# Attention and experts on one core: a large background piece between the two bursts of scores of a step

## The chip, the core and the metric

The kernel runs on one core of a Trainium2 chip. A core has five engines with a queue of instructions each: PE (TensorE, the matrix multiplier; its weight loads are shown apart as PEld), DVE (VectorE), ACT (ScalarE), POOL (GpSimd) and SP (SyncE, which here only issues DMAs). An engine works its queue in order and waits on semaphores for the others. Results of PE land in PSUM, from where DVE and ACT read them; a bank is here a tile of 128 partitions by 512 numbers of 32 bits, and the attention stage uses eight of them. The metric is the time of the kernel on the device in microseconds (us).

## The reference

One transformer layer in 32-bit floats on `x` of 8 batches x 1024 tokens x 256. First causal attention with 16 heads of 16 numbers, then a mixture of 8 experts of which each token uses two:

```python
x = x + layernorm(attention(layernorm(x), Wq, Wk, Wv, Wo))
x = x + layernorm(experts(layernorm(x), router, gate_up, down))

# attention, for each batch and head
score = q @ k.T / sqrt(16)              # 1024 x 1024
score = where(causal, score, -inf)
out = softmax(score) @ v
out = concat_of_heads(out) @ Wo.T

# experts
scores = softmax(flat @ router_weight.T + router_bias)
w, idx = top_k(scores, 2)
gate, up = split(flat @ gate_up[e] + bias[e])       # 512 each
act = (clip(up, -7, 7) + 1) * min(gate, 7) * sigmoid(1.702 * min(gate, 7))
out = sum over the two of w * (act @ down[e] + down_bias[e])
```

The change lies in the attention stage.

## The kernel before

The work of attention is cut into 32 units: 8 batches times 4 groups of 4 heads (`u` in the code, 0 to 31). Softmax needs the maximum of a row before its exponentials, so each unit is gone through twice. In the first pass (`maxima_tiles`, "first" in the loop) PE computes the scores with the queries on the partitions (`sa`, line 686), and DVE reduces them to row maxima (`mx`, lines 696, 702, 711, 717). The maxima are turned by PE (`nmps`, line 655), copied by ACT and put by four DMAs as one more row into the tile of queries (`qP`, line 659), so that the second pass subtracts them in the matrix product itself. In the second pass (`values_tiles`, "second") PE computes the scores again with the keys on the partitions (`sb`, line 781), ACT takes the exponentials (`pT`, line 789), POOL masks the diagonal blocks (line 798), and PE weights the values with them (`av`, line 818). The first pass of unit `u` runs together with the second pass of unit `u - 1`.

A unit has nine steps (`STEPS`, `k` from 0 to 8), which cover the lower triangle of 1024 x 1024 scores. Step kinds are EDGE (a tile with a diagonal block, two DVE reductions), TWO (two partial tiles, with copies by ACT and one more masked reduction) and WHOLE. Each step goes through two pairs of heads, so it has two half steps. A half step begins with a burst of scores: two heads of the first pass and two of the second, each on its own 32 of the 128 rows of PE, so that the four run side by side. Then come the exponentials and reductions of the burst, then half of a weighting: the columns 0 to 255 or 256 to 511 of the step that lies two steps back (`late`), four heads side by side in 32 columns of PE each. One call of `pump` ends the half step.

`pump` puts background work into the loop. This work is written as generators, jobs that yield a `piece` with the time that it is believed to cost PE, DVE, ACT and POOL, and the number of half steps until its input is believed to be ready (`after`). A piece is emitted when it is ready and no engine that it costs has a negative credit; each half step adds credit (0.68 us for PE, capped at 0.9). Three lists are searched in this order: `urgent` (`rows` with `nmps`, `masked_edges`, and `normalize` with `avt`, line 849), the first of `due` (layer norm and transposes of the next batch, its values `vps` in line 577, its projections `pjq` and `pjk` in line 591), then `back` (the output projection `yps` in line 877, the second layer norm, the routing and its scatters). Large pieces cost PE 1.75 us by the kernel's own figures: `vps`, `pjq`, `pjk` and `yps`. All other pieces that use PE are small, 0.6 us at most. Two deadlines, `finish_by`, emit what remains of a batch's values and projections.

The banks of PSUM set limits. `ps_a` has two buffers of two banks for `sa`; `ps_b` has three buffers of one bank, which `sb` (two in each half step), every large piece and every small piece of PE take in turn; `ps_v` has one for `av`. The order of PE, DVE, ACT and SP in the attention stage is the order in which the program emits, and POOL keeps it too (`in_order`).

The experts follow in 71 tiles of 256 tokens (`gu` line 1265, `dn` line 1296), with their own pumping of what is left of attention's last batch.

Of the kernel before, what the change touches and what calls it, by code (L numbers as in the profile page):

```python
# [58 lines left out]
def attn_moe_kernel(  # L59
# [345 lines left out]
    with ExitStack() as attn:  # L405
# [236 lines left out]
        def maxima_tiles(u):  # L642
# [82 lines left out]
            def counted_off(k):  # L725
                for c in {i // n for i, _, _ in STEPS[k][1]}:
                    left[c] -= 1
                    if not left[c]:
                        start(urgent, rows(c))

# [326 lines left out]

        urgent, due, back = [], [], []
        now = 0
        credit = [0.0] * 4  # L1060

        def start(kind, gen):
            job = Job(gen, now)
            kind.append(job)
            return job
# [11 lines left out]

        def pump(*us):

            nonlocal now  # L1080
            for i, more in enumerate(us):
                credit[i] = min(credit[i] + more, 1.3 if i == 3 else 0.9)
            found = True
            while found:
                found = False
                for kind, job in candidates():
                    if job.ready <= now and all(
                        not cost or has >= 0 for cost, has in zip(job.cost, credit)
                    ):
                        for i, cost in enumerate(job.cost):  # L1090
                            credit[i] -= cost
                        emit(kind, job)
                        found = True
                        break
            now += 1
# [22 lines left out]
        with tc.manual_schedule(  # L1118
# [10 lines left out]
            jobs["p1"] = start(due, project(0, 1))  # L1129
            second, late = None, deque()  # L1130
            for u in range(B * NG + 1):
                first = None
                if u < B * NG:
# [9 lines left out]
                    first = maxima_tiles(u)  # L1143
                for k in range(K):
                    if u == B * NG - 1 and not early and NT - LATE in known:
                        load_early()
                    if first and g == 0 and b + 1 < B and k == 5:
                        xs[b + 1] = load_x(b + 1)
                    if first and g == NG - 1 and b + 1 < B and k == K - 2:
                        finish_by(jobs["p0"])  # L1150
                        spread(u + 1)
                        jobs["v"] = start(due, values(b + 1))
                        jobs["p1"] = start(due, project(b + 1, 1))
                    for pair in range(2):
# [14 lines left out]
                        for _, use in reversed(heads):  # L1169
                            use()  # L1170
                        halves = (pair,) if first else (0, 1)
                        if len(late) > DELAY - 1 or (late and not second):
                            f, kk = late[0]
                            for half in halves:
                                f(kk, half)
                            if 1 in halves:
                                late.popleft()
                        if 1 in halves:
                            if first:
                                first[1](k)  # L1180
                            if second:
                                second[1](k)
                                late.append((second[2], k))
                        if first and second:

                            us = 1.64 + 0.62
                            of_dve = {WHOLE: 1.22, EDGE: 1.68, TWO: 0.72}[STEPS[k][0]]
                            of_act = 1.8 if STEPS[k][0] == TWO else 1.2
                            pump(0.68, us - of_dve, us - of_act, us - 0.35)
                        elif first:  # L1190
# [287 lines left out]
```

## Time and profile before

| | |
|---|---|
| Median of 3 runs | 2298.53 us (2292.19 to 2300.28) |
| The profiled execution's own time | 2275.28 us |
| Its span, from the first to the last instruction | 2273.4 us |
| Mean granted TensorE clock | 0.987 of full speed |
| PE busy | 2195.0 us, 97% |
| DVE, ACT, POOL busy | 72%, 48%, 47% |
| Large pieces `vps`, `yps` | 1.99 us each as drawn in the timeline |
| `sb` matmuls, line 781 | 720.0 us busy, 522 ns mean |
| `sa` matmuls, line 686 | 657.0 us busy, 526 ns mean |
| `av` matmuls, line 818 | 366.2 us busy, 368 ns mean |

The attention stage lies in the first 1435 us of the span, the experts in the rest. Each matmul of 32-bit numbers stands in the trace as two passes, so a count of 8 in a row of `av` is four heads. The matmuls of a burst run side by side, and the ends of matmuls are modelled, so the busy times above overlap; what the work takes on PE is read from the start of one group to the start of the next. A group of instructions in the page is given as line, engine, operation, output and input tiles, then busy time and mean duration, then the idle time of the engine before it and what ended that.

### The profile page before, as it was taken

The page shows a single profiled execution, that of the slowest core. Times are in us where ns is not written, and L with a number is a line of the kernel's source. Part 1 is how long each engine was busy: PE and PEld are TensorE (multiplying, and loading weights), DVE is VectorE, ACT ScalarE, POOL GpSimd, SP SyncE. Part 2 cuts the span into 40 slices and gives each one's busy share as a digit, 9 for nine tenths or more (in the row PEclk, how much of TensorE's full clock was granted, in tenths as well). Part 3 has the DMA queues.
Part 4 walks back from the last instruction along what each step waited for, and adds up shares of the span by engine and source line. Part 5 has one row for each costly group of instructions (what it writes and reads, how often), then busy time and mean ns, then how long its engine had stood idle before and what let it go on. Part 6 is the DMA issues. An engine that isn't in the chain of part 4 may idle for free.

```text
span 2273.4 us, 45180 instructions
## 1 busy us (share of the span) xinstructions
PE 2195.0 (97%) x16801; PEld 1363.7 (60%) x16801; DVE 1627.3 (72%) x3677; ACT 1091.8 (48%) x2181; POOL 1070.1 (47%) x1228
## 2 busy tenths in 40 slices
PE   7999999999999999999999999889999999999995
PEld 3444544444444444444445444677888888888884
DVE  4765777777777777777687686665557888887775
ACT  2565665665665666666656656431122323322222
POOL 3321463474364365365365354454444544554543
PEclk9999999999999999999999999999999999999998
DMA  3101102112012013012012010657667877878773
GB/s 81 39 2 39 21 21 58 28 32 58 12 39 48 21 30 86 12 33 55 21 29 58 21 39 30 230 179 221 202 216 256 281 256 268 269 248 279 244 249 110
DMA packets 149106, 251.05 MB, mean 110 GB/s; under 512 B 25920, under 2 KB 111832, under 8 KB 146840
## 3 DMA queue, kind: packets, MB, share of 16 engines
q1 hardware_dynamic: 134168, 210.86, 30.0%
q0 software_dynamic: 12960, 35.47, 4.3%
q8 instruction: 133, 2.18, 0.4%
q10 hardware_dynamic: 1760, 1.84, 0.3%
q14 instruction: 85, 0.70, 0.1%
HBM read 175.66 MB, written 55.68 MB: 102 GB/s over the span
## 4 chain that ended last, share of the span: by engine, by line
PE 83%; DVE 7%; POOL 4%; issue 3%; ACT 1%; DMA 1%; ACTq 0%; POOLq 0%; DVEq 0%; SPq 0%
PE sa L686 19%; PE gu L1265 18%; PE av L818 12%; PE dn L1296 10%; PE sb L781 8%; PE vps L577 3%; PE pjq L591 3%; PE pjk L591 3%; PE yps L877 3%; PE avt L849 1%; PE xtps L1249 1%; POOL pT L798 1%; DVE mx L702 1%; DVE mx L740 1%; DVE sa L696 1%
## 5 line engine op out<-in xcount | busy, mean ns | idle before, releaser
L789 ACT ACTIVATE pT<-sb 128x512 f32<-128x512 f32 x1152 | 625.1, 595 | 348.0 <-PE sb L781 316.8
L781 PE MATMUL sb<-qP,kP 32*128 32x512 f32 (+3 forms) x3072 | 720.0, 522 | 0.5 <-ACT pT L789 0.2
L686 PE MATMUL sa<-kP,qP 32*128 32x512 f32 (+3 forms) x3072 | 657.0, 526 | 6.2 <-DVE mx L702 3.0
L1265 PE MATMUL gu<-xsT,wg 128*128 128x256 f32 x2272 | 520.7, 382 | 2.5 <-ACT xsT L1251 2.5
L1265 PEld LDWEIGHTS gu<-xsT,wg 128*128 128x128 f32 x2272 | 433.9, 191 | 62.8 <-ACT xsT L1251 2.8
L798 POOL TENSOR_SCALAR_AFFINE_SELECT pT<-pT 128x512 f32<-128x512 f32 x256 | 160.3, 642 | 552.8 <-ACT pT L789 368.2
L702 DVE TENSOR_REDUCE mx<-sa 128x2 f32<-128x1024 f32 x256 | 311.5, 1219 | 140.9 <-PE sb L781 137.9
L1276 ACT ACTIVATE sig<-gate 128x256 f32<-128x256 f32 x284 | 118.3, 416 | 569.1 <-DVE gate L1274 540.2
L818 PE MATMUL av<-pT,vpad 128*32 128x256 f32 (+1 forms) x5120 | 366.2, 368 | 1.4 <-DVE avs L829 0.9
L686 PEld LDWEIGHTS sa<-kP,qP 32*128 32x128 f32 x3072 | 229.2, 184 | 207.8 <-issue 133.1
L1281 POOL TENSOR_TENSOR sig<-sig,gate 128x256 f32<-128x256 f32 x284 | 213.4, 753 | 279.8 <-ACT sig L1276 277.7
L781 PEld LDWEIGHTS sb<-qP,kP 32*128 32x128 f32 x3072 | 319.5, 184 | 30.0 <-ACT pT L789 4.6
L818 PEld LDWEIGHTS av<-pT,vpad 128*32 128x32 f32 x5120 | 106.1, 108 | 325.5 <-issue 277.1
L1296 PE MATMUL dn<-wd,act 128*128 128x256 f32 x1136 | 276.2, 384 | 14.1 <-DVE act L1286 14.1
L1274 DVE TENSOR_SCALAR gate<-gu,bs 128x256 f32<-128x256 f32 x284 | 136.0, 479 | 171.6 <-PE gu L1265 156.4
L1296 PEld LDWEIGHTS dn<-wd,act 128*128 128x128 f32 x1136 | 210.8, 192 | 46.5 <-DVE act L1286 21.0
L696 DVE CUSTOM_DVE_ANT_0 sa<-sa,cmask 128x512 f32<-128x512 f32 x256 | 178.3, 696 | 84.4 <-PE sb L781 62.3
L1306 POOL DMA_INDIRECT ytd<-ys,places x142 | 142.6, 1004 | 124.1 <-DVE ys L1302 96.5
L1044 POOL DMA_INDIRECT xsd<-xn,slots x128 | 128.2, 1002 | 107.2 <-DVE xn L1034 46.0
L711 DVE TENSOR_REDUCE mx<-sa 128x2 f32<-128x512 f32 x128 | 88.0, 687 | 88.4 <-PE sb L781 66.1
L1286 DVE SCALAR_TENSOR_TENSOR act<-up,sig 128x256 f32<-128x256 f32 x284 | 124.1, 437 | 21.4 <-POOL sig L1281 21.4
L1278 DVE TENSOR_SCALAR up<-gu,bs 128x256 f32<-128x256 f32 x284 | 134.6, 474 | 0.0
(198 smaller groups left out, 2390.3 us busy)
## 6 DMA issues: line engine op xcount, KB each, us to landing
wg<-_L_ffn_gate_up_proj_dram SPq DMA_DIRECT2D x71, 1024.0 KB
wd<-in_L_ffn_down_proj_dram SPq DMA_DIRECT2D x71, 512.0 KB
xs<-xsd SPq DMA_DIRECT2D x67, 257.0 KB
yy<-ytd SPq DMA_DIRECT2D x16, 1024.0 KB
bs<-biasd SPq DMA_DIRECT2D x71, 132.0 KB
x<-in_L_attn_x_dram SPq DMA_DIRECT2D x16, 512.0 KB
qP<-unq SPq DMA_DIRECT2D x128, 64.0 KB
x1d<-y SPq DMA_DIRECT2D x16, 512.0 KB
```

The source lines that it names most:

```text
L591: nc.tensor.matmul(ps, lhsT=wT[name][:, kt, ts(g2, P)], rhs=xnTs[b][:, kt, ts(c, QC)], start=(kt == 0), stop=(kt == KT - 1),)
L686: nc.tensor.matmul(ps[:, hh, ds(at, w)], lhsT=qP[r, ts(i, P)], rhs=kP[r, ds(c * QC, w)], start=True, stop=True,)
L696: nc.vector.tensor_tensor_reduce(out=ps[:, hh, :], in0=ps[:, hh, :], in1=cmask, scale=1.0, scalar=NEG, op0=ALU.add, op1=ALU.max, accum_out ...
L702: nc.vector.tensor_reduce(mx[:, heads, i, 2:3], ps, AX.X, ALU.max)
L781: nc.tensor.matmul(banks[hh][:, ds(at, QC - off)], lhsT=kP[r, ts(j, P)], rhs=qP[r, ds(c * QC + off, QC - off)], start=True, stop=True,)
L789: nc.scalar.activation(pT[:, 2 * pair + hh, :], banks[hh], AF.Exp)
L798: in_order(nc.gpsimd.affine_select(out=d, in_=d, compare_op=ALU.is_ge, fill=0.0, base=0, pattern=[[0, HG], [1, P]], channel_multiplier=-1,))
L818: nc.tensor.matmul(av[ds(hh * HS, HS), ds(off + a - at, z - a)], lhsT=vp[:, j, ds((g * HG + hh) * VS, HS)], rhs=pT[:, hh, a:z],  start=c n ...
L1265: nc.tensor.matmul(ps[:, half, :], lhsT=wg[:, kt, ds(half * FF + f * P, P)], rhs=xT[:, kt, :], start=(kt == 0), stop=(kt == KT - 1),)
L1281: in_order(nc.gpsimd.tensor_tensor(sg, sg, gt, ALU.mult))
L1296: nc.tensor.matmul(ps[:, n, :], lhsT=act[:, f, ts(n, P)], rhs=wd[:, f, :], start=(f == 0), stop=(f == FT - 1),)
L1306: put = nc.gpsimd.indirect_dma_start(out=yt_dram[:, :], out_offset=bass.IndirectOffsetOnAxis(ap=places[:, i, n : n + 1], axis=0), in_=y[:, ...
```

## The change

In a step with a large piece that can be afforded, the piece now stands between the step's two bursts of scores, where half a weighting stood, and the weighting that was due in the step stands whole behind the second burst. The weighting is kept in halves where it belongs to two chunks of queries (step 2 of a unit). Small pieces are emitted behind the weighting, as before, and large ones no longer are: while both passes run, `pump` takes pieces up to a PE cost of 1.0 only, and in a first half step whose weighting was put off it takes pieces without PE cost only. So there is at most one large piece in a step, always in its first half.

Three smaller edits come with it. Urgent pieces no longer need PE credit. Before each step of the second pass the row maxima that it needs are emitted if they were not yet (`rows_of`). The jobs that compute the next batch's values and its second projections are started at step 5 instead of step 7 of a batch's last unit.

```diff
-                        start(urgent, rows(c))
+                        rows_of[u, c] = start(urgent, rows(c))
...
+        rows_of = {}
...
-        def pump(*us):
-
-            nonlocal now
+        def earn(*us):
             for i, more in enumerate(us):
                 credit[i] = min(credit[i] + more, 1.3 if i == 3 else 0.9)
-            found = True
-            while found:
-                found = False
-                for kind, job in candidates():
-                    if job.ready <= now and all(
-                        not cost or has >= 0 for cost, has in zip(job.cost, credit)
-                    ):
-                        for i, cost in enumerate(job.cost):
-                            credit[i] -= cost
-                        emit(kind, job)
-                        found = True
-                        break
+
+        def affordable(least, most):
+            for kind, job in candidates():
+                if job.ready <= now and least <= job.cost[0] <= most and all(
+                    not cost or has >= 0 or (kind is urgent and not i)
+                    for i, (cost, has) in enumerate(zip(job.cost, credit))
+                ):
+                    return kind, job
+
+        def spend(least=0.0, most=9.0):
+
+
+            found = affordable(least, most)
+            if found:
+                kind, job = found
+                for i, cost in enumerate(job.cost):
+                    credit[i] -= cost
+                emit(kind, job)
+            return found is not None
+
+        def pump(*us, most=9.0):
+
+            nonlocal now
+            earn(*us)
+            while spend(most=most):
+                pass
             now += 1
...
                 for k in range(K):
+                    if second:
+
+                        for c in {t[0] for t in STEPS[k][2]}:
+                            while not rows_of[u - 1, c].done:
+                                emit(urgent, rows_of[u - 1, c])
...
                     if first and g == NG - 1 and b + 1 < B and k == K - 2:
                         finish_by(jobs["p0"])
                         spread(u + 1)
+                    if first and g == NG - 1 and b + 1 < B and k == K - 4:
                         jobs["v"] = start(due, values(b + 1))
                         jobs["p1"] = start(due, project(b + 1, 1))
...
+                        us = 1.64 + 0.62
+                        of_dve = {WHOLE: 1.22, EDGE: 1.68, TWO: 0.72}[STEPS[k][0]]
+                        of_act = 1.8 if STEPS[k][0] == TWO else 1.2
+                        share = 0.68, us - of_dve, us - of_act, us - 0.35
                         halves = (pair,) if first else (0, 1)
+                        if first and second:
+                            earn(*share)
+
+
+                            if pair:
+                                halves = (0, 1) if whole else (1,)
+                            else:
+                                whole = spend(least=1.5) and bool(late) and (
+                                    len({t[0] for t in STEPS[late[0][1]][2]}) == 1
+                                )
+                                halves = () if whole else (0,)
                         if len(late) > DELAY - 1 or (late and not second):
                             f, kk = late[0]
                             for half in halves:
                                 f(kk, half)
-                            if 1 in halves:
+                            if not first or pair:
                                 late.popleft()
-                        if 1 in halves:
+                        if not first or pair:
                             if first:
                                 first[1](k)
                             if second:
                                 second[1](k)
                                 late.append((second[2], k))
                         if first and second:
-
-                            us = 1.64 + 0.62
-                            of_dve = {WHOLE: 1.22, EDGE: 1.68, TWO: 0.72}[STEPS[k][0]]
-                            of_act = 1.8 if STEPS[k][0] == TWO else 1.2
-                            pump(0.68, us - of_dve, us - of_act, us - 0.35)
+                            pump(most=0.0 if whole and not pair else 1.0)
```

More of the change, by code (lines that the diff above doesn't have):

```diff
@@ L1129, in attn_moe_kernel @@
             jobs["p1"] = start(due, project(0, 1))
-            second, late = None, deque()
+            second, late, whole = None, deque(), False
             for u in range(B * NG + 1):
```

## The prediction

> **What bounds the kernel now.** I read the page's busy times first, then its chain, then the attention stage alone.
>
> ```profile
> PE 2195.0 (97%) x16801; PEld 1363.7 (60%) x16801; DVE 1627.3 (72%) x3677; ACT 1091.8 (48%) x2181; POOL 1070.1 (47%) x1228
> ```
>
> ```profile
> PE 83%; DVE 7%; POOL 4%; issue 3%; ACT 1%; DMA 1%; ACTq 0%; POOLq 0%; DVEq 0%; SPq 0%
> ```
>
> ```profile
> 70.00:1435.00 1365.00, 1349.67 (x12815) 649.32 (x12814) 983.26 (x2111) 844.34 (x1629) 644.92 (x715) 1.00 0.14 35
> ```
>
> The third row is the attention stage in the view by windows: length, then busy time of PE, weight loads, DVE, ACT, POOL, clock. TensorE (PE) is never off, the clock is full, the other engines have room. So anything that leaves PE's own order shorter shortens the kernel. But "busy" hides waits: a matmul that waits inside a burst is drawn longer. The timeline of PE shows one:
>
> ```profile
> 1049.97 1.99 PE L577 MATMUL vps<-wvT,xnT 128*128 128x256 f32 x8
> 1051.89 0.70 PE L686 MATMUL sa<-kP,qP 32*128 32x512 f32 x2
> 1051.90 0.70 PE L781 MATMUL sb<-qP,kP 32*128 32x512 f32 x2
> 1052.42 0.59 PE L686 MATMUL sa<-kP,qP 32*128 32x512 f32 x2
> 1052.44 0.59 PE L781 MATMUL sb<-qP,kP 32*128 32x512 f32 x2
> 1052.96 0.64 PE L818 MATMUL av<-pT,vpad 128*32 128x256 f32 x8
> 1053.53 0.70 PE L686 MATMUL sa<-kP,qP 32*128 32x512 f32 x2
> 1053.54 0.91 PE L781 MATMUL sb<-qP,kP 32*128 32x512 f32 x2
> 1054.06 0.59 PE L686 MATMUL sa<-kP,qP 32*128 32x512 f32 x2
> 1054.08 0.80 PE L781 MATMUL sb<-qP,kP 32*128 32x512 f32 x2
> 1054.81 0.64 PE L818 MATMUL av<-pT,vpad 128*32 128x256 f32 x8
> ```
>
> Ends are modelled, so go from start to start. A large piece (`vps`) takes 1.92 us, the burst behind it (four `sa`/`sb` rows) 1.07, a half weighting (`av`) 0.57, the next burst 1.28. The 0.21 extra sits in `sb`. `sb` takes two of the three `ps_b` banks, so its second bank is the one that the first exponential of the burst before must empty; 0.57 us of weighting does not cover that. The exponential itself:
>
> ```profile
> L789 ACT ACTIVATE pT<-sb 128x512 f32<-128x512 f32 x1152 | 625.1, 595 | 348.0 <-PE sb L781 316.8
> ```
>
> ACT idles 316.8 us waiting for scores, so this is a latency loop, not a lack of ACT time. Over units 1 to 31 I took every burst's length minus 1.07 and sorted it by what lay between it and the burst before:
>
> - half weighting alone, the interval before that holding a large piece: 112 bursts, 25.7 us (0.229 each)
> - half weighting alone, otherwise: 163 bursts, 15.1 us (0.093; a burst that waited lets its exponentials start early, so the next hardly waits)
> - half weighting and one, two or three small pieces: 91, 71 and 3 bursts, 0.160, 0.243 and 0.339 each, 32.8 us (a small piece covers 0.59 us but takes a bank, so both exponentials must be done)
> - half weighting and a large piece: 112 bursts, 1.3 us
>
> Together 74.9 us of waiting, 3.3% of the span.
>
> **The change part by part.** The order in which the changed program stands gives the counts. 112 large pieces lie in units 1 to 31 in both. Before, each stood behind a half weighting, 19 of them behind a small piece too. After, all stand directly between the two bursts of a step; in 102 the whole weighting follows the second burst, in 10 (steps whose weighting covers two chunks) the halves stay.
>
> *Waits for banks.* Intervals after: large piece 102, large piece and half weighting 10, whole weighting 86, whole weighting and a small piece 16, half weighting alone 162, with one, two, three small pieces 119, 50, 9. A large piece alone covers 1.92 us. Need: a small piece's 0.57 + 0.59 was short by about 0.2, so both exponentials need some 1.37 us; 1.92 is enough. A whole weighting covers 1.00 us (below), takes no bank, and needs the first exponential only, 0.57 + 0.23 = 0.80 us. So I set both at 0. Of the 162, 36 come behind a whole-weighting interval and start unstalled, so 36 x 0.229 + 126 x 0.093 = 20.0 us. Small ones: 119 x 0.160 + 50 x 0.243 + 9 x 0.339 = 34.2. Rest 0.5. Together 54.7 against 74.9: **-20.2 us**. Bounds: 0 if the waits only move; -30 if bursts behind small pieces profit too. If only the last interval is counted (0.148 for every half weighting alone) it is -15; I take -20, since the split follows the cause.
>
> *Whole weighting.* The last unit, which has no maxima, already weights whole:
>
> ```profile
> 1417.74 1.14 PE L781 MATMUL sb<-qP,kP 32*128 32x512 f32 x8
> 1418.81 1.07 PE L818 MATMUL av<-pT,vpad 128*32 128x256 f32 x16
> 1419.81 0.66 PE L849 MATMUL avt<-ident,avs 128*128 128x128 f32 x4
> ```
>
> Both halves take 1.00 us, two apart 2 x 0.57: 102 x 0.14 = **-14.3 us**. Bounds 0 and -14.3.
>
> *The large piece's new neighbours.* Unit 0 shows burst, large piece, burst without a weighting:
>
> ```profile
> 39.01 1.14 PE L686 MATMUL sa<-kP,qP 32*128 32x128 f32 x8
> 40.08 1.99 PE L577 MATMUL vps<-wvT,xnT 128*128 128x256 f32 x8
> 42.00 1.16 PE L686 MATMUL sa<-kP,qP 32*128 32x128 f32 x16
> ```
>
> 1.07 and 1.92 again. Behind a small piece a large one took 1.81; that is lost 19 times, 2.1 us. Small pieces directly behind a weighting rise from 185 to 197, at 0.59 against 0.53: 0.7 us. **+2.8 us.** Bounds 0 and +5.
>
> The rows carry a price per change between the 32-row, 32-column and full forms: 1.92 - 1.81 = 0.11 us. The Trainium skill, "TensorEngine Tiling (Array Packing)", section Tiling Modes, says that changing the tiling mode drains the engine. By that rule alone one counts changes: 1388 before, 1317 after, 71 x 0.11 = 7.8 us saved instead of 14.3 - 2.8 = 11.5, and the sum would be 3.7 us less of a gain. The trace agrees that a change costs, but the whole weighting's row is closer.
>
> *Urgent pieces without PE credit.* Of 64 `nmps` 35 come one or two half steps earlier, of 64 `avt` 20. PE is in order, so a piece whose DVE input is late holds the next burst and its exponentials. The waits of PE in the attention stage:
>
> ```profile
> PE nmps L655 <- DVE nm L652: 4.1, 5, 1.1
> ```
>
> Those five stood behind the first burst of step 4, where the maxima of two edge steps fill DVE. Of seven at this place before, five waited, 0.82 us each; after there are 16, three behind a large piece, one in unit 0, so 12 that can wait: 12 x 0.82 - 4.1 = **+5.7 us**. Bounds 0 and, with DVE behind in the maxima as well in unit pairs that lose their large pieces from steps 0 to 4 (PE waited 4.0 us for `sa` banks in all), +14. `avt` waited for nothing before; 0, at most the +14 covers it.
>
> *What hangs on others.* ACT's copy of the large piece now stands between the exponentials of the two bursts; it ends 0.6 us into the second burst (1.07), whose exponentials cannot begin earlier: 0, and 0.6 x 102 only if ACT were already late. Scores, copies, DMAs and their number do not change. On SP the four early tile loads (257 KB each) move ahead of the last-but-one unit's `nmT` rows, which are due four half steps (some 7 us) later: 0, at most a few us, once. Values start two steps earlier and are hidden in the same slots. At the seam to the experts (PE idle 19 us of 115) the last routes come slightly earlier; 0, bounds -8 and +8 from its own waits.
>
> **Sum.** -20.2 - 14.3 + 2.8 + 5.7 = -26.0 us. The profiled execution took 2275.3 us (span 2273.4 and 1.9 around it), 1.0% under the median of 2298.5. 2275.3 - 26.0 = 2249.3, a ratio of 0.9886; against the median **2272 us**.
>
> **Rivals.**
> *The waits move rather than go.* PE gets shorter, ACT and DVE do the same work, and the 74.9 us come back elsewhere. For it: DVE is 72% busy in this stage, near full in edge steps. Against: ACT idles for scores, and bursts behind large pieces wait 1.3 us in 112. Time: -11.5 + 5.7 = -5.8, so 2293 us. The Trainium skill, same page, section Performance Considerations, speaks for this: tiling speeds up TensorE but not the emptying of PSUM, which may become the bottleneck. By that rule it would be this rival; ACT's 844 busy of 1365 us speak against.
>
> *Slower: PE waits for DVE at urgent pieces.* 128 `nmps` and `avt` are now emitted when due, whatever PE has spent. Price 0.82 us each. From 31.7 / 0.82 = 39 more late ones on the gain is gone; 45 more late ones add 36.9 to -31.7: 2304 us; all 64 `nmps` late, 2319 us. Against: only 5 of 64 were late, and 27 more moved ones would have to be.
>
> *More than forecast.* No late `nmps`, waits behind small pieces halve with a less loaded bank order, seam 5 us better: about -45, 2253 us.
>
> **How the numbers follow.** A change of 0.5% (11 us) is what a measurement of this kernel tells from none. Forecast 0.65 (2256 to 2286), more than forecast 0.12, waits move 0.16, slower 0.07. The range 2254 to 2294 leaves out part of the second and the last. Faster by over 0.5% (below 2287) 0.79, within 0.14, slower 0.07.
>
> **What would show it.** In the timeline after: burst, large piece at 1.92, burst at 1.07, `av` x16 at 1.00, next burst at 1.07. Attention should end near 1409 instead of 1435, the expert stage stay as long. `sb`'s busy time falls by some 20 us. Wrong if the burst behind a whole weighting is 1.28 again, if a large piece waits for its bank, or if the waits of `nmps` for DVE exceed 30 us.

## The result and the profile after

The change made the kernel faster by less than forecast: 2279.27 us median of 4 runs (2277.76 to 2283.45), against 2297.65 us for the kernel before (median of 4, 2292.19 to 2300.28). The ratio is 0.9926, with a 95% interval of 0.9903 to 0.9949. The forecast was 0.9886, or 2272 us, so about two thirds of the forecast gain came; the time lies inside the stated range.

One thing must be known to read any time here. The chips of this study stand at two levels: on some the kernel before takes about 2274 us, on others about 2296 us. Its profiled execution, on which the prediction was worked out (2275.28 us), fits the first level; the profiled execution of the changed kernel (2283.45 us, span 2281.7 us) fits the second. The two traces may therefore not be subtracted from each other. Ratios below are taken within one chip only, and I call the chips first-level and second-level.

The page of the changed kernel, second level: busy times, the chain, and the group of the exponentials.

```profile
PE 2197.9 (96%) x16801; PEld 1374.6 (60%) x16801; DVE 1634.9 (72%) x3677; ACT 1091.0 (48%) x2181; POOL 1067.7 (47%) x1228
...
PE 83%; POOL 6%; DVE 5%; issue 3%; ACT 1%; DMA 1%; SPq 0%; POOLq 0%; ACTq 0%; DVEq 0%
...
L789 ACT ACTIVATE pT<-sb 128x512 f32<-128x512 f32 x1152 | 625.0, 595 | 433.8 <-PE sb L781 381.3
```

PE bounds it as before. POOL has a larger share of the chain than before (6% against 4%), and ACT idles longer for its scores (381.3 us against 316.8). The attention stage in the view by windows ends near 1440 us here, not near 1409 as forecast:

```profile
70.00:1440.00 1370.00, 1350.49 (x12785) 658.41 (x12783) 995.45 (x2128) 841.42 (x1626) 648.18 (x721) 0.99 0.14 35
```

The order on PE is nevertheless the one forecast, with the forecast times. This is the timeline of PE in a run of the same changed kernel on a first-level chip (`after_third` below):

```profile
772.41 1.99 PE L877 MATMUL yps<-woT,aT 128*128 128x256 f32 x8
774.33 0.70 PE L686 MATMUL sa<-kP,qP 32*128 32x512 f32 x2
774.34 0.70 PE L781 MATMUL sb<-qP,kP 32*128 32x512 f32 x2
774.86 0.59 PE L686 MATMUL sa<-kP,qP 32*128 32x512 f32 x2
774.88 0.59 PE L781 MATMUL sb<-qP,kP 32*128 32x512 f32 x2
775.40 1.07 PE L818 MATMUL av<-pT,vpad 128*32 128x256 f32 x16
776.40 0.70 PE L686 MATMUL sa<-kP,qP 32*128 32x512 f32 x2
776.41 0.70 PE L781 MATMUL sb<-qP,kP 32*128 32x512 f32 x2
776.93 0.59 PE L686 MATMUL sa<-kP,qP 32*128 32x512 f32 x2
776.95 0.59 PE L781 MATMUL sb<-qP,kP 32*128 32x512 f32 x2
777.47 1.99 PE L877 MATMUL yps<-woT,aT 128*128 128x256 f32 x8
```

From start to start: large piece 1.92, burst 1.07, whole weighting 1.00, burst 1.07. Nothing waits here. What went otherwise lies elsewhere, and there are two different things.

**Late consumers, on second-level chips.** In the first trace of the changed kernel eleven bursts are followed by consumers that start 1.6 to 2.1 us after the burst's drawn end; otherwise that is 0.6 us at most in nearly all cases. Here is one. First POOL in the timeline:

```profile
444.90 1.10 POOL L1044 DMA_INDIRECT xsd<-xn,slots  x1 [0.17 <-issue]
446.31 0.96 POOL L1044 DMA_INDIRECT xsd<-xn,slots  x1 [0.30 <-issue]
447.57 0.96 POOL L1044 DMA_INDIRECT xsd<-xn,slots  x1 [0.31 <-issue]
448.84 0.96 POOL L1044 DMA_INDIRECT xsd<-xn,slots  x1 [0.30 <-issue]
```

then ACT beside it:

```profile
447.43 1.08 ACT L789 ACTIVATE pT<-sb 128x512 f32<-128x512 f32 x2 [0.52 <-issue]
451.19 1.09 ACT L789 ACTIVATE pT<-sb 128x512 f32<-128x512 f32 x2 [2.68 <-PE sa L686]
```

PE's burst began at 447.96 and its last score is drawn to 449.20. ACT's exponentials, and at 451.15 DVE's reduction of the same burst, start 2 us later, in the wake of the fourth of four scatters issued in a row (`xsd`, rows of tokens sent to the experts). That the end of the burst is only modelled does not explain it: PE works in order, and its next weighting starts at 449.13 and its next burst at 449.90, both before ACT comes. The same place of the same program on a first-level chip:

```profile
444.13 1.08 ACT L789 ACTIVATE pT<-sb 128x512 f32<-128x512 f32 x2 [0.52 <-PE sb L781]
445.91 1.09 ACT L789 ACTIVATE pT<-sb 128x512 f32<-128x512 f32 x2 [0.69 <-PE sb L781]
```

**Longer waits in few places, on both levels.** I sorted the first-level trace (`after_third`) as the prediction did, every burst's length less 1.07 us:

| bursts of units 1 to 31 | before | after, first level |
|---|---|---|
| waited 0.35 us or less | 526, 59.9 us | 482, 32.4 us |
| waited longer | 27, 15.1 us | 71, 41.7 us |
| together (rounded) | 74.9 us | 74.1 us |

The many small waits fell by 27.5 us, and 26.6 us came back in 44 more long ones.

### The profile page after: what moved, and what is told of

Read it like the earlier page. It is cut to its first block, busy times and chain, and to the rows that moved or that the text cites. A ratio compares the mean times of both kernels' runs of the same rounds, so it can differ in the third digit from the quotient of the medians.

```text
span 2281.7 us, 45149 instructions
## 1 busy us (share of the span) xinstructions
PE 2197.9 (96%) x16801; PEld 1374.6 (60%) x16801; DVE 1634.9 (72%) x3677; ACT 1091.0 (48%) x2181; POOL 1067.7 (47%) x1228
## 4 chain that ended last, share of the span: by engine, by line
PE 83%; POOL 6%; DVE 5%; issue 3%; ACT 1%; DMA 1%; SPq 0%; POOLq 0%; ACTq 0%; DVEq 0%
PE sa L686 19%; PE gu L1296 19%; PE av L818 11%; PE dn L1327 10%; PE sb L781 7%; PE vps L577 3%; PE pjk L591 3%; PE pjq L591 3%; PE yps L877 2%; PE avt L849 1%; PE xtps L1280 1%; POOL pT L798 1%; PE aps L869 1%; POOL xsd L1044 1%; POOL xn L392 1%
## 5 line engine op out<-in xcount | busy, mean ns | idle before, releaser
L789 ACT ACTIVATE pT<-sb 128x512 f32<-128x512 f32 x1152 | 625.0, 595 | 433.8 <-PE sb L781 381.3
L686 PE MATMUL sa<-kP,qP 32*128 32x512 f32 (+3 forms) x3072 | 665.3, 532 | 3.5 <-DVE mx L702 2.2
L818 PE MATMUL av<-pT,vpad 128*32 128x256 f32 (+1 forms) x5120 | 348.5, 369 | 1.5 <-DVE avs L829 0.9
L781 PEld LDWEIGHTS sb<-qP,kP 32*128 32x128 f32 x3072 | 309.5, 186 | 44.7 <-ACT pT L789 15.7
L818 PEld LDWEIGHTS av<-pT,vpad 128*32 128x32 f32 x5120 | 116.8, 109 | 286.4 <-issue 216.7
```

The costliest lines, as they stand in the source:

```text
L686: nc.tensor.matmul(ps[:, hh, ds(at, w)], lhsT=qP[r, ts(i, P)], rhs=kP[r, ds(c * QC, w)], start=True, stop=True,)
L781: nc.tensor.matmul(banks[hh][:, ds(at, QC - off)], lhsT=kP[r, ts(j, P)], rhs=qP[r, ds(c * QC + off, QC - off)], start=True, stop=True,)
L789: nc.scalar.activation(pT[:, 2 * pair + hh, :], banks[hh], AF.Exp)
L818: nc.tensor.matmul(av[ds(hh * HS, HS), ds(off + a - at, z - a)], lhsT=vp[:, j, ds((g * HG + hh) * VS, HS)], rhs=pT[:, hh, a:z],  start=c n ...
```

## The experiments

All times are medians; "late" counts bursts of units 1 to 31 whose first exponential starts more than 1.2 us after the burst's drawn end, in the run's trace; the last column counts runs of scatters on POOL in the attention stage (75 to 1400 us) that start less than 1.6 us after one another.

| run | before beside it | time | ratio (95%) | late | runs of 4 / 8 scatters |
|---|---|---|---|---|---|
| changed, first seen | 2297.65 | 2279.27 | 0.9926 (0.9903 to 0.9949) | 11 | 17 / 0 |
| before_again | 2272.72 | 2273.57 | 1.0002 (0.9989 to 1.0014) | 0 | 9 / 0 |
| halves | 2272.72 | 2287.37 | 1.0067 (1.0051 to 1.0084) | 0 | 17 / 0 |
| urgent_pays | 2272.72 | 2268.28 | 0.9977 (0.9962 to 0.9993) | 0 | 12 / 0 |
| spaced | 2272.72 | 2248.22 | 0.9887 (0.9870 to 0.9903) | 0 | 7 / 3 |
| after_again | 2296.49 | 2274.80 | 0.9911 (0.9886 to 0.9935) | 7 | 17 / 0 |
| spaced_again | 2296.49 | 2293.04 | 0.9983 (0.9967 to 0.9998) | 7 | 6 / 3 |
| before_spaced | 2296.49 | 2292.37 | 0.9982 (0.9964 to 1.0000) | 4 | 6 / 0 |
| after_third | 2275.37 | 2257.46 | 0.9922 (0.9902 to 0.9942) | 0 | 17 / 0 |
| gated | 2275.37 | 2248.02 | 0.9884 (0.9864 to 0.9905) | 0 | 3 / 0, one of 6 |
| before_gated | 2275.37 | 2280.36 | 1.0025 (1.0015 to 1.0034) | 0 | 0 / 0 |
| spread_later | 2293.32 | 2271.36 | 0.9908 (0.9884 to 0.9932) | 11 | 17 / 0 |
| gated_spread | 2293.32 | 2257.12 | 0.9853 (0.9827 to 0.9880) | 3 | 3 / 0 |

**before_again: the kernel before, unaltered.** No edit.

> The kernel before once more, unchanged, with a second trace. Its traced execution took 2275 us, its other runs 2292 to 2300, and the changed kernel's trace (2283 us) shows five stretches of halved TensorE clock in the attention stage where the trace of before has none. Theory A (the trace of before was taken in an unusually good execution): the new trace shows a slower execution, 2290 to 2300 us, with halved clock somewhere in attention. Theory B (the trace was typical, and the times differ for a reason outside the trace): span near 2275 again, full clock from 76 to 1430 us. Ratio to before 1.00 in both.

Measured 1.0002. Its waits are 74.7 us (74.9 in the trace that the prediction used), its attention ends in the same place and no burst is late. So the trace of before was a fair one, for a chip of its level.

**halves: the large piece between the bursts, but the weighting never put off.**

```diff
-                                whole = spend(least=1.5) and bool(late) and (
-                                    len({t[0] for t in STEPS[late[0][1]][2]}) == 1
-                                )
+                                spend(least=1.5)
+                                whole = False
```

> The changed kernel, but the weighting is never put off: large piece between the two bursts, then half a weighting behind each burst as before. Theory 'waits go' (my terms): it loses the whole weighting's 14 us and the waits that 86 + 16 whole weightings covered (about 86 x 0.229 + 16 x 0.2 = 23 us): some 37 us over the changed kernel, 2316 us, above the kernel before. Rival 'waits move': only the 14 us are lost, 2293 us. Rival 'nothing but the urgent rule and the new places matter': 2279 us as the changed kernel.

Measured 1.0067, slower than before. The whole weighting is thus what pays. Against `after_third` (another chip, but of the same level) the stage from unit 1 to unit 32 is 29.8 us longer in the trace: 13.3 us in the weightings themselves (322.7 against 309.4 us) and 18.5 us in waits inside the bursts (92.6 against 74.1 us), less 2 us elsewhere. That is nearer to the 37 us of the first theory than to the 14 us of its rival. Moved without the whole weighting, the large piece takes the cover away from one burst and gives nothing back.

**urgent_pays: urgent pieces need PE credit again.**

```diff
-                    not cost or has >= 0 or (kind is urgent and not i)
+                    not cost or has >= 0
```

> The changed kernel, but urgent pieces need PE credit again as before. Theory (my +5.7 us for row maxima that wait for DVE): 3 to 8 us faster than the changed kernel, 2272 to 2276 us, and the wait of nmps for DVE falls to 4 us. Rival: the exemption costs nothing, 2279 us, or it is needed, 2285 us and more.

Measured 0.9977, less gain than the whole change has on another first-level chip (0.9922), so the expected 3 to 8 us did not come. The waits of `nmps` for DVE did fall, from 4.8 us in `after_third` to 2.9, but waiting for credit makes the row maxima late. PE in the timeline of this version, then its windows:

```profile
246.74 1.83 PE L781 MATMUL sb<-qP,kP 32*128 32x256 f32 x4 [2.53 <-DMA qP<-nmT]
```

```profile
244.00:246.00 2.00, 0.21 (x2) 0.00 (x0) 0.91 (x3) 0.00 (x0) 2.00 (x3) 1.00 0.01 2
246.00:250.00 4.00, 3.26 (x15) 1.68 (x16) 0.00 (x0) 1.63 (x3) 1.73 (x2) 0.51 0.01 3
250.00:254.00 4.00, 4.00 (x35) 2.19 (x37) 3.02 (x6) 1.28 (x3) 0.12 (x1) 0.63 0.02 4
```

The granted clock (the third number from the end of a window) falls to half 1.9 us into this wait of 2.53 us and stays there for 6.8 us. It happens twice, the other time in a wait of 2.57 us. So urgent pieces cost something with credit and without, and without is the better of the two.

**spaced: every scatter's piece becomes ready one half step after the last.** This was made against the late consumers, when the two levels were not yet known.

```diff
-                    yield piece(pool=1.1, after=0 if n else 1)
+                    yield piece(pool=1.1, after=1)
```

> The changed kernel, but the four scatters of a token block are at least one half step apart. In the trace of the changed kernel eleven bursts get their exponentials 1.6 to 2.1 us late, all of them ending 0.3 to 0.6 us after the start of the fourth of four scatters that POOL issued without a break, and the halved clock follows some of them. Theory (the unbroken scatters do it): the eleven late bursts and most of the halved clock in attention disappear, 11 x 1.6 = 18 us plus some 8 us of clock: 2253 to 2264 us. Rival (the place in the batch does it, not the scatters): late bursts stay, 2275 to 2285 us. Rival (the scatters come later and the last batch's routes with them): 2285 us and more.

Measured 0.9887, what had been forecast for the change. But the trace did not bear out the reason: POOL still issued runs of four, now even three runs of eight, and in the same place as one late burst of the first trace the lag was 0.21 us. POOL has little to wait for between scatters, so emitting them apart does not space them in time. That no burst was late is a matter of the chip, as the next runs show. The ratio is not that alone: the unaltered change, on a first-level chip and without a late burst, gave 0.9922 (`after_third` below). Against that trace the stage of `spaced` is 5.2 us shorter and what follows it 4.2 us; which pieces fell into better half steps was not followed.

**after_again, spaced_again, before_spaced: the same programs on another chip.** `before_spaced` has the edit of `spaced` in the kernel before.

> The changed kernel unaltered, on the same chip as the runs beside it. Theory A (the eleven bursts whose consumers start 1.6 to 2.1 us late, and the stretches at half clock, belong to this program's order of instructions): the ratio to the kernel before is again about 0.993 (2256 us where before takes 2272), and the same eleven places (the second burst of step 6 or the first of step 0, 3.1 us after the first of four scatters) show the lag. Theory B (they belong to the chip or the execution on which the changed kernel was first seen, since at 430.8 us the version with the scatters' pieces pushed on has the same four scatters, the same burst 3.14 us behind the first, and a lag of 0.21 us): the ratio is about 0.988 to 0.989 (2245 to 2248 us), no burst is late by over 1 us, and no clock is halved between 76 and 1400 us; then pushing the scatters on was worth nothing by itself.

> The version whose scatters each wait for one more call, once more beside the changed kernel. By theory A it stays 7 to 12 us below the changed kernel; by theory B the two are within 3 us of each other. Either way some 0.9885 of the kernel before (2247 us where before takes 2272).

> The kernel before with only the scatters' pieces pushed on by one call each. Theory A and theory B both expect no change, since no burst of the kernel before is followed by late consumers: within 4 us of before. A rival, that pushing the scatters on by itself spreads POOL's and the queues' work and is worth something in any order, expects 8 to 15 us less than before.

This chip was of the second level. `after_again` gives 0.9911, with seven of the eleven late bursts in the same places, which is nearer to theory A. `spaced_again`, the same program as `spaced`, loses nearly all its gain: 0.9983, which neither theory had. Both theories were wrong in taking all chips for alike. `before_spaced` is 4.1 us below before, about the 4 us that both theories allowed. The windows of `spaced` and of `spaced_again` over a run of eight scatters, one program on two chips:

```profile
908.00:912.00 4.00, 4.00 (x52) 1.47 (x51) 1.92 (x3) 2.08 (x4) 2.78 (x3) 1.00 0.27 71
912.00:916.00 4.00, 4.00 (x32) 1.71 (x30) 2.32 (x3) 2.68 (x6) 2.97 (x4) 1.00 0.29 101
916.00:920.00 4.00, 4.00 (x32) 1.43 (x34) 2.21 (x4) 2.42 (x5) 1.92 (x2) 1.00 0.28 100
```

```profile
924.00:928.00 4.00, 4.00 (x48) 1.40 (x44) 1.23 (x1) 1.09 (x2) 3.08 (x4) 1.00 0.36 102
928.00:932.00 4.00, 1.12 (x4) 0.29 (x2) 0.00 (x0) 0.00 (x0) 3.09 (x4) 0.78 0.29 102
932.00:936.00 4.00, 0.06 (x1) 0.06 (x1) 1.82 (x2) 0.70 (x2) 1.07 (x2) 0.50 0.18 66
936.00:940.00 4.00, 4.00 (x14) 1.36 (x14) 0.63 (x1) 1.47 (x3) 0.00 (x0) 0.50 0.00 0
```

On the first chip PE, DVE and ACT work on beside POOL's eight scatters. On the second DVE stands idle for 8.2 us and ACT for 9.8 although PE had finished their burst by 926.4, PE runs out of banks, and its clock halves. DVE goes on at 933.8, 1.4 us after the last of the eight scatters began at 932.4. The two spans are 2248.5 and 2293.9 us.

**after_third, gated, before_gated: scatters that have to wait for DVE.** In the gated versions DVE copies the row numbers of each scatter into a tile of its own, one half step after the other, so that POOL cannot issue the next scatter before DVE has come by.

```diff
-                    yield piece(pool=1.1, after=0 if n else 1)
+                    yield piece(after=1)
+                    go = ap2.tile([P, 1], I32, tag=f"go{r}{n}", name=f"go_{t}_{r}_{n}")
+                    nc.vector.tensor_copy(go, sf[:, r, n : n + 1])
+                    yield piece(pool=1.1)
...
-                        out_offset=bass.IndirectOffsetOnAxis(ap=slots[:, t, r, n : n + 1], axis=0),
+                        out_offset=bass.IndirectOffsetOnAxis(ap=go, axis=0),
```

> The changed kernel unaltered, beside its version with gated scatters. Two kinds of chip have been seen: one on which the kernel before takes some 2272 us and no burst is late, and one on which it takes some 2296 us and bursts that fall into four or more scatters in a row are followed by late consumers. Theory (consumers learn of PE's work late while POOL issues scatters in a row, on the second kind of chip alone): on the first kind 0.988 to 0.990 of before (2245 to 2250 us) and no late burst; on the second kind 0.991 to 0.993 (2275 to 2280 us) with 7 to 13 late bursts. Rival (lateness belongs to single executions, not to the chip): 0.991 on either kind.

> The changed kernel with each scatter's row numbers copied by DVE into a tile of its own one call before it, so that POOL can issue the four scatters of a group only as DVE comes past the four copies, some 2 us apart instead of 1.27 us. It adds 8 copies of some 0.16 us on DVE for each of the 32 tables' token blocks, 41 us of DVE work in all, beside PE's work. Theory: no burst is late by more than 1 us on either kind of chip; 2245 to 2260 us on both, so 0.989 to 0.993 of before on the first kind and 0.978 to 0.984 on the second, 15 to 30 us below the changed kernel there. Rival (lateness has another cause, such as the queue or the chip's memory): the late bursts stay on the second kind of chip and the time is within 6 us of the changed kernel's, or above it by what DVE's copies cost.

> The same gate in the kernel before. Theory: on the second kind of chip it loses what that chip adds, 2270 to 2282 us (0.988 to 0.994); on the first kind there is nothing to lose, 2270 to 2280 us (1.000 to 1.003). The change measured between the two gated kernels is then 0.987 to 0.992 on either kind, the forecast's 0.9886 among them. Rival: within 4 us of before on either kind.

The chip was of the first level. `after_third` has the same 17 runs of four scatters and not one late burst, so runs alone do not make consumers late; the chip has to be of the second level. But it gave 0.9922, not the 0.988 to 0.990 of the theory: on this level, too, a third of the forecast gain is missing, and late consumers have no part in it. `gated` gave 0.9884 with no lateness to cure, so what it gains over `after_third`, 9.4 us, has another cause. It has 71.2 us of waits against 74.1, and its stage is 5.4 us shorter, since its pieces fall into other half steps; 3.9 us of it lie in a place that the next runs look at, the rest was not followed. In the kernel before the gate costs 0.25%, so between the two gated kernels the change is worth 0.9858 (2248.02 against 2280.36), more than the 0.987 to 0.992 expected.

**spread_later, gated_spread: the next unit's queries and keys sent later.** In the trace of `after_third` seven first bursts of step 2, one in every fourth unit, were too long, 9.0 us together and 1.3 us or more in six of them; in the trace of before the same seven lost 1.4 us together. The timelines of PE and of SP there:

```profile
452.76 0.60 PE L686 MATMUL sa<-kP,qP 32*128 32x256 f32 x4
453.42 1.28 PE L781 MATMUL sb<-qP,kP 32*128 32x256 f32 x4
```

```profile
435.83 8.92 SPq L612 DMA_DIRECT2D qP<-zeros  x2
444.80 2.97 SPq L617 DMA_DIRECT2D qP<-unq  x4
447.81 2.49 SPq L617 DMA_DIRECT2D kP<-unk  x4
450.40 2.52 SPq L659 DMA_DIRECT2D qP<-nmT  x4
```

ACT had turned the maxima into `nmT` by 447.1. Their four DMAs stand on SP behind eight that bring the next unit's queries and keys, and these behind two that zero a row of the same tile and wait for PE's last scores from it. So the four go out from 450.4 to 452.9, and PE, which now comes round sooner, waits for them. In six of the seven units it reaches step 2 now 7.6 us after the unit's first burst, before 9.6 to 10.5 us, because a large piece and transposes (`xps`) stood in between. The weight loads show the wait:

```profile
PEld sb L781 <- DMA qP<-nmT: 5.1, 12, 0.7
```

The edit, alone in the changed kernel and in the gated one:

```diff
-                    if g < NG - 1:
-                        spread(u + 1)
...
+                    if first and g < NG - 1 and k == 4:
+                        spread(u + 1)
```

> The changed kernel with the copies of the next unit's queries and keys (SP's eight or more DMAs of some 0.62 us each) issued at step 4 of a unit instead of at its start. In the changed kernel's trace on a chip without late bursts (before 2275 us there, this change 2257 us) seven first bursts of step 2, one in every fourth unit, are 1.3 us too long, 9.0 us together, and end when the row maxima's DMAs land, which SP issues right behind those copies; PE's weight loads wait 5.1 us for these DMAs. Theory (the row maxima come late because SP's queue is longer than what PE now takes to come round): 8 to 12 us below the changed kernel, so 0.987 to 0.989 of before (2245 to 2250 us against 2275), with no first burst of step 2 over 0.6 us too long and less than 2 us of waiting for the row maxima's DMAs. Rival (another engine takes over as soon as these are gone, DVE's reductions or the exponentials): within 4 us of the changed kernel, 0.991 to 0.993, the waits now at the next bursts. On a chip with late bursts (before 2296 us) some 20 us of stalls stay in both, so 0.986 to 0.990 by the theory.

> The same later copies in the version whose scatters wait for DVE one by one. There four such bursts lose 5.1 us. Theory: 4 to 8 us below 0.9884 of before, so 0.985 to 0.987 (2241 to 2246 us against 2275) on a chip without late bursts, and 0.976 to 0.981 on one with them, since the gate keeps consumers from being late there (nothing over 1 us). Rival: 0.988 to 0.990 on the first kind; and if the gate doesn't help, 0.985 to 0.995 on the second.

The chip was of the second level. In `spread_later` the maxima go out at once,

```profile
443.80 2.60 SPq L659 DMA_DIRECT2D qP<-nmT  x4
446.45 1.26 SPq L612 DMA_DIRECT2D qP<-zeros  x2
447.77 2.49 SPq L617 DMA_DIRECT2D qP<-unq  x4
```

and the waits at that place are gone: the ten first bursts of step 2 behind a half weighting alone waited 0.92 us each in `after_third` and 0.10 here, and PE waits for no `nmT` DMA any more. The two traces come from different levels, though, and on second-level chips the unaltered change had less to lose there: 0.24 us each when first seen and 0.45 in `after_again`. There a late burst at step 0 of the same unit can hold PE up and so give SP time: when first seen, five of the units had one and lost 0.22 us at most at step 2, and unit 6, which had none, lost 1.39. So the cause of the 9.0 us is shown by the DMAs' times in `after_third` and agrees with this run; that 9.0 us would be saved on a first-level chip was not tried. The ratio here is 0.9908, within the interval of `after_again` and just above the 0.986 to 0.990 expected. `gated_spread` has the best ratio of all, 0.9853, some 36 us below before. Its expectation was missed on both counts: 0.976 to 0.981 was too much (0.9853 lies at the edge of the rival's range), and it still has three late bursts. These three stand, each, at one of the three runs of four scatters that the gate left (two token blocks in flight at once; the timeline of POOL):

```profile
563.23 0.96 POOL L1047 DMA_INDIRECT xsd<-xn,go  x1 [0.68 <-DVE go L1045]
564.50 0.96 POOL L1047 DMA_INDIRECT xsd<-xn,go  x1 [0.30 <-issue]
565.77 0.96 POOL L1047 DMA_INDIRECT xsd<-xn,go  x1 [0.30 <-DVE go L1045]
567.04 0.96 POOL L1047 DMA_INDIRECT xsd<-xn,go  x1 [0.31 <-issue]
568.98 0.96 POOL L1047 DMA_INDIRECT xsd<-xn,go  x1 [0.98 <-issue]
```

The late burst begins at 568.0, just after the run that started at 563.23, and its exponentials start at 570.6, after the single scatter that follows. On one chip the gate took late bursts from 11 to 3 and long runs from 17 to 3, and where runs stayed, lateness stayed. Not all of its gain comes from that: the gate is worth 14.2 us here (2271.36 to 2257.12) and 9.4 us on the first level, where no burst was late.

## Why the prediction was right and where it failed

The direction was right, and so was one of the two large terms, the whole weighting. The other, the waits for banks, failed, and the size with it. The prediction's sum was made on a trace of the first level, so `after_third` answers it. Stage and span there against the trace of before: unit 1 to unit 32 took 1311.7 us against 1328.6, the span is 2255.3 against 2273.4, 18.1 us shorter where 26.0 was forecast.

| step of the prediction | forecast | measured, first level |
|---|---|---|
| waits for banks, inside the bursts | -20.2 (54.7 of 74.9) | -0.8 (74.1) |
| whole weighting | -14.3 | -13.3 (322.7 in `halves` to 309.4) |
| waits behind the weightings | none | -6.3 (329.0 before to 322.7 in `halves`) |
| the large piece's new neighbours | +2.8 | +2.6 (large pieces +1.5, small ones +1.1) |
| urgent pieces, PE waiting for DVE at `nmps` | +5.7 | +0.7 (4.1 to 4.8) |

The waits of the last row lie mostly in the third row already; the first four rows give -17.8, near the 16.9 of the stage.

**Neighbours:** right in sum, to 0.2 us.

**Whole weighting:** right. `halves` has the large pieces in the same place and no whole weighting, so its weightings less those of `after_third` are what merging is worth: 13.3 us, 0.13 for each of 102. The whole weighting takes the forecast 1.00 us (102 at 1.003).

**Waits behind the weightings:** in all, the weightings became 19.6 us shorter (329.0 to 309.4), and 6.3 us of that were gone in `halves` too, where nothing is merged. From start to start a half takes 0.594 us on average in the trace of before, but 528 of 554 take the 0.57 of the rows quoted. The other 26 take up to 1.75 us, because what stands behind them on PE waits, mostly for DVE, as in this timeline of before:

```profile
1350.03 0.64 PE L818 MATMUL av<-pT,vpad 128*32 128x256 f32 x8
1351.33 0.70 PE L686 MATMUL sa<-kP,qP 32*128 32x512 f32 x2 [0.65 <-DVE mx L702]
```

In `halves` and in `after_third` 14 weightings are drawn out so. The prediction had no term for these waits but the one at `nmps`, and let that rise. Why the others fell was not followed.

**Urgent pieces:** over-priced. Six `nmps` waited for DVE, 4.8 us together, not the twelve of the forecast. In the rival of this kind, all 64 late would give 2315 us, not 2319, since 4.1 us of it are in the kernel before already.

**Waits for banks:** the step that failed, by 19.4 us. Its two boldest lines hold: the 102 bursts behind a large piece alone waited 0.2 us together and the 86 behind a whole weighting 0.2 us, as set. What failed is the line that carried old prices over to the classes that remain: half weighting alone 30.5 us against 20.0, small pieces 42.7 against 34.2. The prices were means over classes, and the change moved within a class what the price depends on. The new waits have two places, the first explained and the second not:

- 9.0 us at the first burst of step 2, behind the row maxima's DMAs, as the timelines above show. The prediction had looked at SP's queue only for four early tile loads, and not for the eight DMAs that stand ahead of the maxima. What had covered them in these units were a large piece and transposes on PE, some 2 to 3 us.
- 8.9 us at the bursts with `nmps` ahead of them: 61 such bursts before and after, 13.2 us against 22.1. An `nmps` is 0.2 us of PE but takes a bank, and ACT empties it behind both exponentials. Such a piece stands alone behind a weighting 28 times now and 25 before (9.1 us against 6.6), with one of the next batch's transposes (`xps`) 6 times and 2 before (3.9 us against 0.6), and with `avt` 15 times and 18 before, at 0.47 us each now and 0.27 before. That these pieces move earlier was counted in the prediction (35 of 64), but only PE's wait for DVE was priced. Yet that move does not explain most of the 8.9 us: in `urgent_pays`, where `nmps` needs credit again, the 61 bursts wait 27.9 us, and still 19.2 without the two that wait 4.4 us each for late maxima; in `halves` they wait 20.0 us. So most of the rise belongs to something that all three versions share, such as the large pieces' new place; no run took that away, and its cause stays open.

Without these two, 17.9 us, the waits would be 56.2 us, close to the 54.7 forecast; that is a sum and not a run.

That two thirds of the gain came all the same is partly luck: the miss of 19.4 us was made up for in part by waits for DVE. The forecast let them rise by 5.7 us, and the waits behind the weightings, which are mostly for DVE, fell by 6.3.

**Rivals.** "The waits move rather than go" is half true. The sum of the waits for banks did not fall (74.9 to 74.1), but the waits behind the weightings fell, and those for DVE at urgent pieces did not rise as that rival, like the forecast, had them, so the ratio is 0.992, between its 2293 us and the forecast's 2272. The Trainium skill, "TensorEngine Tiling (Array Packing)", section Performance Considerations, had been read as speaking for it, with the emptying of PSUM as the next bound. The traces agree only in that ACT's copies and exponentials hold the banks; ACT itself idles more than before for scores (409.8 us of idle time ahead of the exponentials in `after_third`, 348.0 before), so it is order, not ACT's capacity. "Slower: PE waits for DVE at urgent pieces" is refuted in its own form, 4.8 us on the first level and 7.3 on the second.

**By counting tiling modes**, the rule taken from the Trainium skill, same page, section Tiling Modes, weightings and neighbours together gave 7.8 us; measured are 10.7 (13.3 less 2.6), and the forecast had 11.5. The merged weighting's own row was the better guide.

**The seam and the experts:** from unit 32 on 871.5 us against 872.5, within the forecast 0 and its bounds.

**What no step had:** late consumers. On the second level they lengthen the changed kernel's stage (1311.7 us in `after_third`, 1320.2 in `after_again`, 1329.4 when first seen). They hardly show in the ratio, because the kernel before is some 22 us slower there as well. What it loses there is open: no trace of it, unaltered, was taken on such a chip; `before_spaced`, near to it, has four late bursts, and 5.1 us are lost to its halved clock between 80 and 1380 us.

## What to carry to other kernels

When work is taken out of an in-order engine, look next at every queue that ran beside it with time to spare, DMA queues too: what was just in time (here the row maxima behind eight other DMAs) is late as soon as the engine comes round sooner. A mean wait of a class of intervals may be carried over to the new order only if what lies inside the class stays. A time from start to start holds the wait of whatever stands next: compare the mean with the usual value (0.594 and 0.57 us here) before pricing with it. And time a candidate on several chips before believing a few tenths of a per cent: `spaced` was 1.1% faster than before on one chip and 0.2% on the next.

## What the runs showed of the hardware that was not expected

- On some chips, while POOL issues four or more indirect DMAs within 1.3 us of one another, ACT and DVE start late on a finished burst, mostly only after POOL has issued the last of the run: 1.4 to 3.6 us late at runs of four, 3.0 to 9.0 us at runs of eight. On others the same programs show nothing of it (0.61 us at most in `after_third`, `spaced` and `gated`). Not every run of four has a late burst, 11 of 17 at most, and two late bursts of `before_spaced` (1.5 and 1.3 us) lay beside runs of only two. Why the chips differ, and what holds ACT and DVE back, stays open. Each chip was seen at one time only, so that its level is a lasting property of the chip is not shown.
- The clock fell to half in waits of PE shorter than expected: 2.53 and 2.57 us in `urgent_pays`, 1.9 and 2.3 us after the drawn end of the last matmul, for 6.8 us each time. The Trainium skill, "TensorE: Matmul & The Clock Gate", the table in Part 1's section What's actually happening, puts the fall after an idle window of about 3.4 us; here a gap drawn shorter than that sufficed. In the first trace of the changed kernel three of the late bursts were followed by the same, here where the drawn wait was only 0.81 us:

```profile
451.00:453.00 2.00, 1.19 (x6) 0.58 (x4) 1.80 (x5) 1.21 (x4) 0.00 (x0) 1.00 0.59 103
453.00:455.00 2.00, 2.00 (x18) 0.93 (x20) 1.85 (x7) 1.09 (x2) 0.84 (x2) 0.65 0.63 105
455.00:457.00 2.00, 2.00 (x22) 0.93 (x14) 0.65 (x1) 0.54 (x2) 2.00 (x3) 0.50 0.02 3
```

The drawn PE busy time of 1.19 us in the first of these windows leaves just those 0.81 us idle. Since the ends of matmuls are modelled, the true gap may have been longer; its length cannot be read exactly. Summed over windows of 2 us between 80 and 1380 us, the halved clock takes 9.3 us in that trace, 18.7 us in `spaced_again` and nothing in `after_third`.
